# A graph-attention layer on one core: 16 rows a group by the sync engine in place of 8, and another order of the steps of a group

## The chip, the cores and the metric

The kernel runs on one core of a Trainium2 chip. The metric is device time in microseconds (us) of one execution. Three runs of the kernel before gave 2603.59, 2608.92 and 2620.65 us; the median, 2608.92 us, is the number that a change is measured against. One more execution was taken by the hardware profiler. It took 2620.06 us, and all rows, views and stage times below come from it.

The core has five instruction streams that wait for each other through semaphores: TensorE (PE; its weight loads are shown as PEld), VectorE (DVE), ScalarE (ACT), GpSimd (POOL), which issues indirect gathers, and SyncE (SP), which issues plain loads and stores.

## What is computed

The reference is one attention layer over a graph of 12500 nodes with 128 features and 212500 edges that are sorted by their destination, with two normalizations behind it:

```python
Q = (x @ WQ).reshape(N, H, dh)            # N = 12500, H = 8, dh = 16
K = (x @ WK).reshape(N, H, dh)
V = (x @ WV).reshape(N, H, dh)
Eh = (edge_attr @ WE).reshape(-1, H, dh)  # 212500 edges
score = K[src] * Q[dst] / jnp.sqrt(jnp.float32(dh)) * Eh
score = jnp.exp(jnp.clip(score.sum(-1, keepdims=True), -5.0, 5.0))
msg = V[src] * score
wV = jax.ops.segment_sum(msg, dst, num_segments=N)
Z = jax.ops.segment_sum(score, dst, num_segments=N)
h = x + (wV / (Z + ATTN_EPS)).reshape(N, D)
# batch norm of h over the nodes, then layer norm of x + that over the features
```

## The kernel before

**Tiles and stages.** Edges are cut into 1661 tiles of 128, and these into 208 groups of 8 tiles (the last has 5). A group is two half-groups of four tiles, and the destinations of a half lie in a window of 64 nodes, since edges are sorted. The kernel first projects all nodes to a table of K and V in DRAM (`kvd`, one row of 1 KB a node). Then one loop runs over the groups (lines 815 to 865), and a short stage normalizes and stores.

**What a group needs.** K and V rows of its 1024 sources come by indirect gathers on POOL, one per tile of 128 edges (`gather`, line 223), into one of nine slots of SBUF, some eight groups ahead. `load` (line 505) brings the 512 KB of edge features by SP, four groups ahead, into one of three buffers `ea`. Q of the destinations is made by PE from two windows of node columns: `q_window` (ACT copies, line 532), `q_mm` (PE, 563), then `q_hi`, `q_mid`, `q_lo` (ACT, DVE and ACT, DVE), which split the result into three bf16 parts.

**The steps of a group**, with the line of the instruction in the profile:
- `ehqe` (before) projects the edge features, PE line 582 into the PSUM tile `ps_e`, copies them to `wt` by ACT (584), and spreads Q over the edges by six bf16 matmuls, PE 590 into `ps_q`, with the turned one-hot `ot` (DVE 553) as the other operand.
- `both` (DVE 595) multiplies the two; `turn_back` (PE 603, eight transposes into `ps_t`) puts edges on partitions.
- `products` (DVE 616) multiplies with K, `scores` (DVE 623) sums each head, `clip_exp` clips (DVE 631) and makes the exponentials twice on ACT (632 into PSUM, 633 into `msg`).
- `message` (DVE 641) multiplies V with the exponentials; `onehot` (DVE 543, 545, 546) compares destinations with a ramp `iota_ps`; `gather_sum` (PE 656, 657) sums messages by destination; `sums_out` (ACT 662) takes the sums out of PSUM.
- `denom`, `recip`, `attn` (DVE 666, 669, 673) divide; `add_x` (PE 682, 683) adds x; `x_out` (ACT 687) writes the result to the node columns `hx`.

**One PSUM tile is shared.** `small_ps` (`ps_m` in the profile, one bank) holds Q's product, the result of `add_x`, the ramp `iota_ps` and the two sets of exponentials, a quarter each.

**Order.** The schedule is written out by hand: each engine runs its instructions in the order in which the loop calls the steps, for groups from g-3 to g+4 in one pass. Nothing is reordered. A call that must wait holds up all that stands behind it on its engine.

**What paces the gathers.** When `message` has read a slot, `load_kv` queues the gathers of a later group into it. In the next pass `pace` (line 234) lets the first queued gather wait for `q_mm` of that pass, and `issue` gives POOL the rest at once.

**Rows by SP.** The last tile of some groups is not gathered by POOL. SP fetches its 128 rows one at a time: `fetch_rows` (line 271) loads the byte offsets of `SP_ROWS` rows into registers (line 276) and issues as many DMAs of 1 KB (line 283) into a tile `byrow`. It is called in each pass from group 3 on, between the loads and the steps. `row_plan` (line 61) finds which groups get a tile in this way: with 8 rows a group a tile takes 16 groups, and the groups are 20, 36, ..., 196, 12 in all; they gather 7 tiles by POOL. Their last tile has products and messages of its own (`parts`, line 263), behind a wait for the rows (`rows_there`).

Of the kernel before, what the change touches and what calls it, by code (L numbers as in the profile page):

```python
# [8 lines left out]
F32 = mybir.dt.float32  # L9
# [3 lines left out]
AF = mybir.ActivationFunctionType  # L13
# [4 lines left out]
P = 128  # L18
# [4 lines left out]
U = 4  # L23
# [7 lines left out]
FIRST_ROW = 3  # L31
LATE = 8
ROW_LAG = 2
SP_ROWS = 8
WORDS = 4
RQ = 4
NSEM = 6
# [23 lines left out]
def row_plan(sizes):  # L61


    full, n = sizes.count(U) // 2, SP_ROWS
    groups, end = [], P
    while FIRST_ROW + -(-end // n) - 1 + ROW_LAG < full:
        groups.append(max(NX, FIRST_ROW + -(-end // n) - 1 + ROW_LAG))
        end += P
    assert sorted(set(groups)) == groups
    return groups  # L70
# [7 lines left out]
def gnn_kernel(  # L78
# [19 lines left out]
    nc = tc.nc  # L98
# [4 lines left out]
    NG = NW // 2  # L103
# [11 lines left out]
    psp = pps.enter_context(tc.tile_pool(name="psum", bufs=1, space=bass.MemoryType.PSUM))  # L115
# [53 lines left out]
    def load_last():  # L169
        nc.scalar.dma_start(rel_i[:, cut:], dst[:, cut:])  # L170
        nc.scalar.dma_start(srcs[:, cut:], src[:, cut:])
        nc.scalar.dma_start(gb[:, 0:1], gamma)
        nc.scalar.dma_start(gb[:, 1:2], beta)
# [34 lines left out]
    def slot(i):  # L208
        return rows.tile([P, 2 * G * P], F32, name=f"slot{i}")
# [19 lines left out]
    def issue(n=0):  # L229
        while len(queued) > n:  # L230
            f, *a = queued.pop(0)
            f(*a)

    def pace(step):
        if queued:
            f, *a = queued.pop(0)
            tc.add_manual_dep(f(*a).ins, step.ins.name,
                              mybir.DependencyInfo(mybir.DependencyClass.Sync, mybir.DependencyReason.DATA),
                              reason="pace")
# [4 lines left out]
    row_loads = []  # L244
    n = SP_ROWS
    row_tiles = row_plan(usizes)
# [24 lines left out]
    def fetch_rows(g):  # L271
        if g not in fill:
            return
        q = fill[g]
        c = q // P * cols
        _, offs = nc.values_load_multi_w_load_instructions(
            row_ids[q % P:q % P + 1, c:c + cols], engines=(ET.SP,), min_val=0, max_val=(N - 1) * 8 * P,
            skip_runtime_bounds_check_because="node ids")
        for r, off in zip(range(q * n, min(q * n + n, tot)), offs):
            k = row_tiles[r // P]  # L280
            if r % P == 0:
                by_row[k] = rows.tile([P, 1, 2 * P], F32, name="byrow", bufs=2)
            d = nc.sync.dma_start(by_row[k][r % P:r % P + 1, 0, :].bitcast(U8), kvb[ds(off, 8 * P)].unsqueeze(0))
            d.then_inc(rows_in[r // P % NSEM], 16)
            tc.no_tile_sem_insts.add(d.ins.name)
            tc.add_to_no_dep_group(f"rows{k}", d.ins)
# [21 lines left out]
    for g in range(nxg):  # L308
        if g % 2 == 0:
            PAIR[g // 2] = free.pop(0)  # L310
            t = slot(PAIR[g // 2])
# [41 lines left out]
    def within(f, g):  # L353
        return f(g) if 0 <= g < NG else None
# [47 lines left out]
    def load_quad(q):  # L402
        t = late[0].tile([P, RQ, U * P], BF16, name="rbq", bufs=2)
        for h in (0, 1):
            at = ustarts[2 * RQ * q + h] * P
            nc.sync.dma_start(t[h * WN:(h + 1) * WN], bass.AP(
                tensor=relT.tensor, offset=relT.offset + at, ap=[[0, WN], [G * P, RQ], [1, U * P]]))
        for k in range(RQ):
            RB[RQ * q + k] = t[:, k, :]
# [87 lines left out]
    EA, OH, OT, Q3, XW, BASE, MSG, QE, OS, AT, AGG, WT, PW = ({} for _ in range(13))  # L497

    def nt(g):
        return sizes[g]  # L500

    def halves(g):
        return [(0, usizes[2 * g]), (usizes[2 * g], nt(g))]
# [7 lines left out]
    def project_main(g):  # L511

        half = [table_tile(2 * (g % 2) + a) for a in (0, 1)]
        KV[g] = lambda a, b, c, n=P: half[a // 4][:, a % 4:a % 4 + b - a, c:c + n]
        turn_x(g, 0, True)
        turn_x(g, 4, True)
        yield
        for a in (0, 4):
            project(g, a, lambda: turned().rearrange("p (a b) d -> p a (b d)", b=2), True)
            yield  # L520
# [13 lines left out]
    def onehot(g):  # L534


        n, m = usizes[2 * g], usizes[2 * g + 1]
        t = wp.tile([P, U * P + U * WN], F32, name="oh", bufs=2)
        one = t[:, :n * P].rearrange("p (a b) -> p a b", b=P)
        two = t[:, U * P:U * P + m * WN].rearrange("p (a b) -> p a b", b=WN)  # L540
        OH[g] = [one[:, j, :] for j in range(n)] + [two[:, j, :] for j in range(m)]
        r = rel[:, starts[g]:starts[g] + nt(g)]
        nc.vector.tensor_tensor(one, iota_ps[:, None, :].to_broadcast([P, n, P]),  # L543
                                r[:, :n, None].to_broadcast([P, n, P]), op=OP.is_equal)
        nc.vector.tensor_scalar(one[:, :, WN], r[:, :n], lim[:, 2 * g:2 * g + 1], None, op0=OP.is_equal)
        nc.vector.tensor_tensor(two, iota_ps[:, None, :WN].to_broadcast([P, m, WN]),  # L546
                                r[:, n:, None].to_broadcast([P, m, WN]), op=OP.is_equal)
# [26 lines left out]
    def q_lo(g):  # L574
        nc.vector.tensor_sub(Q3[g][:, 2, :], QR[g], Q3[g][:, 1, :])

    def ehqe(g):

        QE[g], WT[g] = [], []
        for a, b in halves(g):  # L580
            eh = psp.tile([P, U * P], F32, name="ps_e", bufs=2)[:, :(b - a) * P]
            nc.tensor.matmul(eh, w_e, EA[g][:, a:b, :].rearrange("p a b -> p (a b)"), start=True, stop=True)  # L582
            t = wp.tile([P, U * P], F32, name="wt", bufs=2)
            nc.scalar.activation(t[:, :(b - a) * P], eh, AF.Copy)  # L584
            WT[g].append(t)
            QE[g].append(psp.tile([P, U * P], F32, name="ps_q", bufs=2)[:, :(b - a) * P])
        for k in range(3):
            for h, (a, b) in enumerate(halves(g)):
                r = slice(h * WN, (h + 1) * WN)
                nc.tensor.matmul(QE[g][h], Q3[g][r, k, :], OT[g][r, :(b - a) * P], start=(k == 0), stop=(k == 2))  # L590

    def both(g, h):
        a, b = halves(g)[h]
        t = WT[g][h][:, :(b - a) * P]
        nc.vector.tensor_tensor(t, t, QE[g][h], op=OP.mult)  # L595
# [165 lines left out]
    q_mid(2)  # L761
    turn_back(0)
    ehqe(1)
    nc.vector.tensor_scalar(row_ids, row_ids, 8 * P, None, op0=OP.mult)
    onehot(0)
    within(load, 2)
    turned_onehot(2)
    load_rel(3)
# [10 lines left out]
    def bn_parts(a, b):  # L779
        for w in range(a, b):  # L780
            for j in due.get(w, []):
                bn_part(j)
                done.add(j)
# [22 lines left out]
    def within_checks(g):  # L806
        if g >= first_check and (g - first_check) % every == 0:
            check((g - first_check) // every)
# [6 lines left out]
    for g in range(NG - 2):  # L815
        within(load, g + 4)
        within(load_rel, g + 5)
        if (g + 6) % RQ == 0 and (g + 6) // RQ in quads:
            load_quad((g + 6) // RQ)
        fetch_rows(g)  # L820
        within(products, g)
        within(both_halves, g + 1)
        step = within(add_x, g - 3)
        step = within(q_mm, g + 3) or step
        if step is not None and queued and g >= LATE + 4:
            pace(step)
        issue()
        within(gather_sum, g - 1)
        if g + 1 < nxg and g + 1 not in SLOT:
            for _ in project_main(g + 1):  # L830
                pass
        within(turn_back, g + 1)
        within(scores, g)
        within(clip_exp, g)
        within(q_hi, g + 3)
        within(x_out, g - 3)
        within(sums_out, g - 1)
        within(q_lo, g + 2)
        within(denom, g - 2)
        within(recip, g - 2)  # L840
        within(attn, g - 2)
        within(q_window, g + 4)
        within(turned_onehot, g + 3)
        within(ehqe, g + 2)
        within(q_mid, g + 3)
        within(message, g)
        within(onehot, g + 1)
        if g == 2:
            load_last()
        for r in runs[1:]:  # L850
            if g == max(4, r[0] // 2 - 12):
                place(r)
        within_checks(g)
        while free and todo and not pending:
            load_x()
        bn_parts(2 * g - 5, 2 * g - 3)
        if g == NG - 5:
            assert done >= set(range(NPRE))
            norm_first()
        if g == LATE - 1:  # L860
            tps.close()
            late.append(tps.enter_context(tc.tile_pool(name="late", bufs=1)))
        if g == LATE - 2:
            free.append(NSLOT)
            load_kv()
    last = NG - 1
    g = last - 1
# [328 lines left out]
```

## Time and profile before

| | |
|---|---|
| median of three runs | 2608.92 us (2603.59 to 2620.65) |
| the profiled execution, own time | 2620.06 us |
| its span, first to last instruction | 2618.3 us |
| mean granted TensorE clock | 0.889 |
| busy: PE, DVE, POOL, ACT | 1833.5, 1659.3, 1589.8, 641.8 us |
| gathers of K and V by POOL | 1585 |
| rows by SP | 1536 |
| first exponential (line 632) to last | 111.8 to 2570.5 us |

A row of the timeline gives the start in us, the time that the instruction or the merged run of instructions took, engine, line, operation, tiles out<-in and a count, and in brackets the idle time of the engine before it with what ended it. A row of the waits gives who waited, for whom, the sum in us, the number of times and the longest. A row of the groups of instructions gives after the count the busy time and the mean ns of one, then the idle time just before them and what ended most of it. A row of the stages gives each engine's busy time in a stretch, the granted clock, the share of the DMA engines' time and GB/s. "remote" and "issue" name waits whose end the profile puts on no engine.

### The profile page before, as it was taken

To read this page: it belongs to the slowest core of one execution; us is meant where nothing else is said; L and a number is where in the kernel's file an instruction comes from. 1 tells how busy PE (TensorE), PEld (TensorE's weight loads), DVE (VectorE), ACT (ScalarE), POOL (GpSimd) and SP (SyncE) were. 2 spreads that over 40 slices of the span, in tenths; PEclk is the share of its full clock that TensorE was granted. 3 is DMA by queue.
4 is the path that set the end of the run, shared out by engine and by line. 5 is a ranking of instruction groups with operands and counts; after the bars stand their busy time and mean duration, and the time that the engine had idled before them with its cause. 6 is when DMAs were issued, how large, how long until landed. Compare 5 with 4: busy or idle time off the path is not lost. (4 is left out here: it accounts for less than half of the span.)

```text
span 2618.3 us, 34368 instructions
## 1 busy us (share of the span) xinstructions
PE 1833.5 (70%) x9414; PEld 1171.7 (45%) x9414; DVE 1659.3 (63%) x3577; ACT 641.8 (25%) x2480; POOL 1589.8 (61%) x1685
## 2 busy tenths in 40 slices
PE   6668676767776676666767677677666776767577
PEld 5445444444444444343444444444434444444346
DVE  2335666666666666666666566666666666666587
ACT  2223222222222222222222222222222222222235
POOL 6644566666666666666666656666666666666524
PEclk8879799888889889999888989988988998799899
DMA  7733444544445444454544544545445454454454
GB/s 229 243 110 110 135 146 147 145 148 145 148 138 154 146 144 148 140 155 137 155 146 138 148 141 144 147 147 145 148 135 155 137 156 137 148 149 140 132 173 118
DMA packets 175392, 386.61 MB, mean 148 GB/s; under 512 B 37518, under 2 KB 91831, under 8 KB 175191
## 3 DMA queue, kind: packets, MB, share of 16 engines
q0 software_dynamic: 78128, 212.05, 27.6%
q1 hardware_dynamic: 92900, 169.50, 21.3%
q10 hardware_dynamic: 4163, 2.78, 0.4%
q8 instruction: 77, 1.26, 0.2%
q14 instruction: 124, 1.02, 0.1%
HBM read 364.57 MB, written 19.63 MB: 147 GB/s over the span
## 5 line engine op out<-in xcount | busy, mean ns | idle before, releaser
L223 POOL DMA_INDIRECT slot<-kvd,srcs x1585 | 1501.3, 947 | 914.6 <-issue 433.2
L657 PE MATMUL ps_a<-msg,oh 128*128 128x136 f32 (+1 forms) x3322 | 609.3, 330 | 5.5 <-issue 4.5
L582 PE MATMUL ps_e<-ea,w_e 128*128 128x512 f32 x832 | 479.6, 648 | 176.5 <-issue 165.5
L657 PEld LDWEIGHTS ps_a<-msg,oh 128*128 128x128 f32 (+1 forms) x3322 | 496.5, 194 | 99.2 <-issue 80.7
L595 DVE TENSOR_TENSOR wt<-wt,ps_q 128x512 f32<-128x512 f32 x416 | 278.2, 685 | 370.7 <-remote 133.8
L632 ACT ACTIVATE ps_m<-s 128x64 f32<-128x64 f32 (+1 forms) x209 | 47.5, 227 | 1497.7 <-PE ps_e L582 541.5
L682 PE MATMUL ps_m<-ident,at 128*128 128x128 f32 x412 | 107.3, 347 | 382.1 <-DVE oh L546 137.6
L603 PE MATMUL ps_t<-ident,wt 128*128 128x128 f32 x1661 | 249.7, 288 | 121.4 <-issue 64.9
L582 PEld LDWEIGHTS ps_e<-ea,w_e 128*128 128x128 f32 x832 | 157.5, 203 | 351.1 <-issue 340.8
L584 ACT ACTIVATE wt<-ps_e 128x512 f32<-128x512 f32 x416 | 236.5, 595 | 249.9 <-PE ps_q L590 130.1
L682 PEld LDWEIGHTS ps_m<-ident,at 128*128 128x128 f32 x412 | 70.1, 213 | 475.6 <-issue 239.3
L571 DVE SCALAR_TENSOR_TENSOR qr<-ps_m,q 128x128 f32<-128x128 f32 x208 | 60.2, 289 | 345.3 <-ACT hx L687 318.6
L616 DVE TENSOR_TENSOR p<-slot,ps_t 128x512 f32<-128x512 f32 (+1 forms) x410 | 259.9, 675 | 19.6 <-remote 13.1
L603 PEld LDWEIGHTS ps_t<-ident,wt 128*128 128x128 f32 x1661 | 194.4, 147 | 152.4 <-issue 77.9
L623 DVE TENSOR_REDUCE s<-p 128x64 f32<-128x1024 f32 (+1 forms) x209 | 252.0, 1206 | 0.1
L641 DVE TENSOR_TENSOR msg<-slot,ps_m 128x1024 f32<-128x1024 f32 (+2 forms) x209 | 246.4, 1181 | 0.4 <-ACT ps_m L632 0.3
L590 PE MATMUL ps_q<-ot,q 64*128 64x512 bf16 x1248 | 177.5, 390 | 5.3 <-issue 5.0
L543 DVE TENSOR_TENSOR oh<-ps_m,rel_i 128x512 f32<-128x512 f32 x208 | 142.2, 684 | 46.7 <-remote 39.8
L590 PEld LDWEIGHTS <-q 64*128 64x128 bf16 x1248 | 46.5, 95 | 199.4 <-issue 175.5
L673 DVE SCALAR_TENSOR_TENSOR at<-os,keep,rz 128x128 f32<-128x128 f32 x208 | 73.3, 352 | 37.2 <-PE ps_t L603 12.0
L563 PE MATMUL ps_m<-w_q,xw 128*128 128x128 f32 x416 | 94.6, 315 | 1.8 <-DVE oh L543 1.6
L687 ACT ACTIVATE hx<-ps_m 128x64 f32 x412 | 90.3, 219 | 8.0 <-PE ps_m L683 1.2
(173 smaller groups left out, 1601.7 us busy)
## 6 DMA issues: line engine op xcount, KB each, us to landing
ea<-eaT SPq DMA_DIRECT2D x207, 512.0 KB
slot<-kvd,srcs POOLq DMA_INDIRECT x1585
byrow<-kvd SPq DMA_DIRECT2D x1536, 1.0 KB
rbq<-relT SPq DMA_DIRECT2D x94, 256.0 KB
kvd<-slot SPq DMA_DIRECT2D x12, 512.0 KB
kvd<-t SPq DMA_DIRECT2D x12, 512.0 KB
slot<-xT SPq DMA_DIRECT2D x24, 256.0 KB
out<-o SPq DMA_DIRECT2D x23, 256.0 KB
```

What stands on the lines that cost most here:

```text
L223: return nc.gpsimd.indirect_dma_start(out=out, out_offset=None, in_=table, in_offset=bass.IndirectOffsetOnAxis(ap=srcs[:, e:e + 1], axis=0))
L543: nc.vector.tensor_tensor(one, iota_ps[:, None, :].to_broadcast([P, n, P]), r[:, :n, None].to_broadcast([P, n, P]), op=OP.is_equal)
L582: nc.tensor.matmul(eh, w_e, EA[g][:, a:b, :].rearrange("p a b -> p (a b)"), start=True, stop=True)
L584: nc.scalar.activation(t[:, :(b - a) * P], eh, AF.Copy)
L590: nc.tensor.matmul(QE[g][h], Q3[g][r, k, :], OT[g][r, :(b - a) * P], start=(k == 0), stop=(k == 2))
L595: nc.vector.tensor_tensor(t, t, QE[g][h], op=OP.mult)
L603: nc.tensor.transpose(ps[:, j, :], WT[g][h][:, j * P:(j + 1) * P], ident)
L616: step = nc.vector.tensor_tensor(PR[g][:, c:d, :], KV[g](c, d, 0), PW[g][i][:, c - a:d - a, :], op=OP.mult)
L623: nc.vector.tensor_reduce(SS[g][:, a:b, :], PR[g][:, a:b, :].rearrange("p t (h d) -> p t h d", d=DH), axis=AX.X, op=OP.add)
L641: step = nc.vector.tensor_tensor(MSG[g][:, a:b, :P].rearrange("p t (h d) -> p t h d", d=DH), KV[g](a, b, P).rearrange("p t (h d) -> p t h ...
L657: nc.tensor.matmul(AGG[g][WN if j >= n else 0:], OH[g][j], MSG[g][:, j, :], start=(j == 0), stop=(j == n - 1))
L682: nc.tensor.matmul(ps, AT[g], ident, start=True, stop=False)
```

## The change

`SP_ROWS` is 16 in place of 8. By `row_plan` a tile is then complete in 8 groups; the groups that have one are 12, 20, ..., 204, 25 in all, and rows are fetched in groups 3 to 202. `ehqe` is cut in three (`eh_mm` on PE, `eh_out` on ACT, `qe_mm` on PE), and the pass calls its steps in another order.

```diff
-SP_ROWS = 8
+SP_ROWS = 16
...
-    def ehqe(g):
-
-        QE[g], WT[g] = [], []
+    EH = {}
+
+    def eh_mm(g):
+
+        EH[g] = []
         for a, b in halves(g):
             eh = psp.tile([P, U * P], F32, name="ps_e", bufs=2)[:, :(b - a) * P]
             nc.tensor.matmul(eh, w_e, EA[g][:, a:b, :].rearrange("p a b -> p (a b)"), start=True, stop=True)
+            EH[g].append(eh)
+
+    def eh_out(g):
+        WT[g] = []
+        for h, (a, b) in enumerate(halves(g)):
             t = wp.tile([P, U * P], F32, name="wt", bufs=2)
-            nc.scalar.activation(t[:, :(b - a) * P], eh, AF.Copy)
+            nc.scalar.activation(t[:, :(b - a) * P], EH[g][h], AF.Copy)
             WT[g].append(t)
-            QE[g].append(psp.tile([P, U * P], F32, name="ps_q", bufs=2)[:, :(b - a) * P])
+
+    def qe_mm(g):
+        QE[g] = [psp.tile([P, U * P], F32, name="ps_q", bufs=2)[:, :(b - a) * P] for a, b in halves(g)]
         for k in range(3):
             for h, (a, b) in enumerate(halves(g)):
                 r = slice(h * WN, (h + 1) * WN)
                 nc.tensor.matmul(QE[g][h], Q3[g][r, k, :], OT[g][r, :(b - a) * P], start=(k == 0), stop=(k == 2))
+
+    def ehqe(g):
+        eh_mm(g)
+        eh_out(g)
+        qe_mm(g)
...
     nc.vector.tensor_scalar(row_ids, row_ids, 8 * P, None, op0=OP.mult)
-    onehot(0)
     within(load, 2)
...
         fetch_rows(g)
         within(products, g)
+        within(q_lo, g + 2)
         within(both_halves, g + 1)
         step = within(add_x, g - 3)
         step = within(q_mm, g + 3) or step
         if step is not None and queued and g >= LATE + 4:
             pace(step)
         issue()
+        within(x_out, g - 3)
+        within(q_window, g + 4)
+        within(q_hi, g + 3)
         within(gather_sum, g - 1)
+        within(eh_mm, g + 2)
         if g + 1 < nxg and g + 1 not in SLOT:
             for _ in project_main(g + 1):
                 pass
         within(turn_back, g + 1)
         within(scores, g)
         within(clip_exp, g)
-        within(q_hi, g + 3)
-        within(x_out, g - 3)
         within(sums_out, g - 1)
-        within(q_lo, g + 2)
         within(denom, g - 2)
         within(recip, g - 2)
         within(attn, g - 2)
-        within(q_window, g + 4)
         within(turned_onehot, g + 3)
-        within(ehqe, g + 2)
+        within(onehot, g)
         within(q_mid, g + 3)
+        within(eh_out, g + 2)
+        within(qe_mm, g + 2)
         within(message, g)
-        within(onehot, g + 1)
+        if g == NG - 3:
+            onehot(g + 1)
```

So on PE the edges' projection stands between `gather_sum` and `turn_back`; on ACT the copies of `x_out`, `q_window` and `q_hi` stand ahead of the exponentials; on DVE the one-hot of a group is made in that group's own pass, ahead of `q_mid` and `message`, and no longer in the pass before, behind `message`; and `q_lo` stands ahead of `both`.

## The prediction

> **What bounds the kernel now.** I read the page's busy times and groups first, then the timelines of POOL, ACT and SP around one pass, then the waits, and last the stages with and without gathers.
>
> ```profile
> PE 1833.5 (70%) x9414; PEld 1171.7 (45%) x9414; DVE 1659.3 (63%) x3577; ACT 641.8 (25%) x2480; POOL 1589.8 (61%) x1685
> ...
> L223 POOL DMA_INDIRECT slot<-kvd,srcs x1585 | 1501.3, 947 | 914.6 <-issue 433.2
> ...
> L595 DVE TENSOR_TENSOR wt<-wt,ps_q 128x512 f32<-128x512 f32 x416 | 278.2, 685 | 370.7 <-remote 133.8
> ```
>
> No engine is full. So the bound is a chain, and the timeline of POOL shows which: eight gathers 1.25 us apart, then a pause; the group with a `byrow` tile has seven.
>
> ```profile
> 1424.02 0.94 POOL L223 DMA_INDIRECT slot<-kvd,srcs  x1 [0.30 <-issue]
> 1427.13 1.00 POOL L223 DMA_INDIRECT slot<-kvd,srcs  x1 [2.17 <-remote]
> 1428.44 0.94 POOL L223 DMA_INDIRECT slot<-kvd,srcs  x1 [0.30 <-issue]
> ...
> 1434.70 0.95 POOL L223 DMA_INDIRECT slot<-kvd,srcs  x1 [0.30 <-issue]
> 1437.52 0.94 POOL L223 DMA_INDIRECT slot<-kvd,srcs  x1 [1.88 <-PE ps_e L582]
> ```
>
> The same three passes on ACT, by the start of the exponential:
>
> ```profile
> 1415.04 0.23 ACT L632 ACTIVATE ps_m<-s 128x64 f32<-128x64 f32 x1 [7.87 <-PE ps_e L582]
> 1426.90 0.23 ACT L632 ACTIVATE ps_m<-s 128x64 f32<-128x64 f32 x1 [7.87 <-PE ps_t L603]
> 1437.28 0.23 ACT L632 ACTIVATE ps_m<-s 128x64 f32<-128x64 f32 x1 [6.47 <-PE ps_e L582]
> 1449.10 0.23 ACT L632 ACTIVATE ps_m<-s 128x64 f32<-128x64 f32 x1 [7.40 <-remote]
> ```
>
> A pass with eight gathers takes 11.86 and 11.82 us, the one with seven 10.38. Over the loop (300.5 to 2507.8 us, 188 passes, by the starts of line 632) the 149 passes with eight gathers have a median of 11.83 us, and 1494 gathers take 2207.3 us, 1.48 us each. POOL and the exponential start 0.23 us apart because both wait for `q_mm`: POOL by `pace`, the exponential because it writes to the same PSUM tile. The record of `q_mm` itself stands 7.6 us earlier (line 563 at 1301.00, exponential at 1308.62). So its completion is seen late, about when the last gather of the burst is through, 2.6 to 2.9 us after that gather's start. The cycle is: `q_mm` seen, burst of gathers, burst through, next `q_mm` seen. Where no gather runs, a pass takes 7.52 us and DVE is full:
>
> ```profile
> 2518.20:2540.70 22.50, 18.91 (x121) 12.27 (x120) 21.84 (x49) 8.17 (x33) 0.00 (x0) 1.00 0.65 207
> 1320.40:1344.10 23.70, 16.40 (x86) 10.53 (x86) 15.35 (x34) 5.41 (x22) 15.13 (x16) 0.93 0.43 134
> ```
>
> The columns after the length are PE, PEld, DVE, ACT and POOL busy, clock, DMA share and GB/s. Compute has over 4 us of air in a pass beside gathers. SP, which is to do twice the rows, shows two speeds:
>
> ```profile
> 1322.91 0.36 SPq L508 DMA_DIRECT2D ea<-eaT  x1
> 1324.15 8.01 SPq L283 DMA_DIRECT2D byrow<-kvd  x8
> 1334.73 0.36 SPq L508 DMA_DIRECT2D ea<-eaT  x1
> ...
> 1485.55 0.36 SPq L508 DMA_DIRECT2D ea<-eaT  x1
> 1485.96 1.25 SPq L406 DMA_DIRECT2D rbq<-relT  x2
> 1488.35 3.68 SPq L283 DMA_DIRECT2D byrow<-kvd  x8
> 1509.24 0.36 SPq L508 DMA_DIRECT2D ea<-eaT  x1
> 1510.49 1.55 SPq L283 DMA_DIRECT2D byrow<-kvd  x5
> ```
>
> In the middle of a burst eight rows take 8.0 us (6.5 and 7.6 in the two passes before), 0.8 to 1.0 each; at the start of one five take 1.55, 0.31 each.
>
> **The change part by part.** The sum is made on the profiled execution's 2620.06 us (span 2618.3), which lies 0.43% over the median of 2608.92; I apply the difference to the median.
>
> *Gathers.* 25 groups in place of 12 have a tile by rows: 13 gathers fewer. One is worth the 1.25 us of POOL's own spacing at least, and at most the 1.48 us of the mean; the difference of the two kinds of pass, 11.83 - 10.38 to 10.51, is 1.32 to 1.45. I take 1.40: 13 x 1.40 = -18.2 us (ends -16.3 and -19.2).
>
> The Trainium skill (DMA: Bandwidth & Descriptors, "Issuing engines are not separate DMA queues") says that DMAs from any engine end on the same 16 DMA engines, and that spreading them saves only issue time. By that the 13 x 128 rows cost as much from SP, and the sum would be 0 in place of -18.2. The seven-gather pass disagrees: its 128 rows are moved too, and it is 1.4 us shorter.
>
> *Rows on SP.* 1664 more row issues, 8 more in each of 192 passes and 16 in 8 more. SP's pass then is one load (0.36), a register load (0.73, perhaps twice that for 16 values), a quarter of 1.25 for `rbq`, and 16 rows. At 0.31 a row that is 6.4 us, at 1.0 a row 17.4. The slow stretch is some 7.1 us of a pass and takes 7 to 9 rows; the other 7 to 9 take 2.2 to 2.8 us. Sum 7.1 + 2.5 + 1.4 = 11.0 us, 11.7 with two register loads. That is under 11.83, so I take nothing, but barely. Behind SP's rows stand the next `ea` load and `rbq`; `ea` is used two passes (23 us) after its issue, and a tile of rows two passes after its last row, so some us of lateness are hidden. If SP needs more than a pass, that cover is used up, and the excess is paid in every pass. The rows' 1 KB transfers I take at nothing, since the pass of 21.3 us at 1492.0 and the others keep the same 1.4 us a gather.
>
> *Edges ahead.* The four records of line 582 move ahead of eight transposes; PE's work is the same. `load` waits for the end of line 582 to free an `ea` buffer (1322.91, 2.5 us after the exponential). Now the transposes no longer stand ahead: 0.8 to 1.6 us earlier. That is the start that SP's sum above needs, and itself worth nothing while SP isn't the bound. The transposes are late by 4 x 0.43 us of PE, where PE waits for DVE 595 in any case.
>
> *ACT.* Two copies of `x_out` (0.47), two of `q_window` (0.40) and `q_hi` (0.26) now run between `q_mm` and the exponential, which so starts 0.9 to 1.3 us after `q_mm` is seen. This is on the way to `message`.
>
> *One-hots and DVE.* `message` starts 1.2 us after the exponential now, and products 3.5. The one-hot (0.68 + 0.23 + 0.42, 1.33 us) leaves the place behind `message`. It reads the ramp in `ps_m`, and waits on that tile go by the whole tile:
>
> ```profile
> PE ps_m L682 <- DVE oh L546: 137.6, 73, 3.4
> ```
>
> PE waits there for a one-hot that reads another quarter. So I take it that the one-hot waits for the exponential. Then exponential until 1.3, one-hot 2.65, `q_mid` 2.95, `message` 4.15: products start 0.65 us later than now. If it needn't wait, 0.6 us earlier. `q_lo` adds 0.28 ahead of `both`. Behind these stands DVE 595, which waits 0.89 us a time now (370.7 / 416), at some 6 us into the pass; the lateness goes there. `q_mm` is issued at about 4.9 us in place of 4.2, and is seen at 11.8 either way: 0. Without that cover it would be +0.65 us a pass, 120 us. The split tiles of 13 more groups add some 0.3 us each on DVE, 4 us, in the same air.
>
> Sum: -18.2 us. 2620.06 becomes 2602 in a profiled execution, and the median 2590.7.
>
> **The rivals.**
>
> *The pause shrinks.* A pass is about 1.41 us a gather and 0.54 us besides (11.83 = 8 x 1.41 + 0.54). In the burst four completions of PE are seen ahead of `q_mm`'s: two of line 590, those of 682 and 683. Edges first and SP at work from early on could let them through sooner, and POOL would not stop. Against it: where POOL ran through, two passes took 7.42 and 21.26 us (exponentials at 1484.6, 1492.0 and 1513.3), 28.7 us for 19 gathers, and the formula gives 27.9. All of it gone: 0.54 x 187 = 101 us, 2490; half, 2540.
>
> *SP becomes the bound.* This one ends slower. If the register load is double and a row in the slow stretch costs 1.0 us, 7 rows fit there, 7.1 + 9 x 0.31 + 2.13 = 12.0, and with waits for line 582 perhaps 12.25: +0.42 us in 175 passes, 73 us, less 18: 2664. It decides from 11.83 us of SP work a pass on. For it: the spread of 6.5 to 8.0 us for 8 rows; against it: SP waits some 2 us a pass for line 582 now.
>
> *The gathers' transfers bound, not their issue.* Then nothing is won: 2609. The seven-gather passes speak against it.
>
> **How the numbers follow.** The forecast (gathers gone, pass unchanged) has 0.43, with a range of its own of 2576 to 2604; the shrinking pause 0.31; SP as the bound 0.18; no effect 0.08. A measurement of this kernel can tell about 1% from no change: 2583 to 2635. Faster by over 1% takes the shrinking pause and 0.05 of the forecast's own range, 0.36; slower takes SP's case and 0.02 of the forecast, for the 0.65 us on DVE where its cover fails, 0.20; within 1% the rest, 0.44. The range leaves out a tenth on each side: from 2525, beyond half the pause, to 2665, SP's price.
>
> **What would show it.** Right: exponentials 11.8 us apart in passes of eight gathers, 25 passes of some 10.4 us, 1572 gathers, products about 4 us after `q_mm` is seen, `ea` loads some 1 us earlier. Wrong: passes of eight gathers under 11.6 us (the pause), or over 12 us with SP issuing rows without a break and `ea` or `byrow` waited for on PE or DVE. A first gather that starts well before the burst ahead of it is through would make my cycle wrong as such.

## The result, and the profile after

The changed kernel took 2738.52 us (median of four executions, 2729.05 to 2744.09) against 2607.14 us for the kernel before (four executions): 1.0489 times, with a 95% interval of 1.0457 to 1.0521. It is slower by 131 us, and outside the range of the prediction. The profiled execution took 2729.05 us (span 2727.3), 109.0 us more span than the profiled execution before.

The page's groups first. Lines are now those of the changed kernel: the exponential is 646, `products` 630, `both` 609, `eh_mm` 584.

```profile
PE 1906.1 (70%) x9414; PEld 1285.0 (47%) x9414; DVE 1659.0 (61%) x3603; ACT 680.0 (25%) x2480; POOL 1575.0 (58%) x1672
...
L223 POOL DMA_INDIRECT slot<-kvd,srcs x1572 | 1486.5, 946 | 1020.5 <-issue 392.9
...
L609 DVE TENSOR_TENSOR wt<-wt,ps_q 128x512 f32<-128x512 f32 x416 | 268.5, 683 | 397.7 <-remote 179.8
...
L630 DVE TENSOR_TENSOR p<-byrow,ps_t 128x128 f32<-128x128 f32 x25 | 7.2, 287 | 222.3 <-DVEq L290 148.2
```

13 gathers are gone (1585 to 1572), yet POOL is idle ahead of them for 1020.5 us in place of 914.6. The last line is new among the costly groups: ahead of the 25 products that read a tile of rows, DVE is idle for 222.3 us, 8.9 us each. Line 290 is the wait for the rows. Before, the 12 such products waited for nothing:

```profile
L616 DVE TENSOR_TENSOR p<-byrow,ps_t 128x128 f32<-128x128 f32 x12 | 3.4, 280 | 0.0
```

One such pass after the change on ACT, by the start of the exponential:

```profile
1357.13 0.23 ACT L646 ACTIVATE ps_m<-s 128x64 f32<-128x64 f32 x1 [1.31 <-DVE rz L680]
...
1369.04 0.23 ACT L646 ACTIVATE ps_m<-s 128x64 f32<-128x64 f32 x1 [1.52 <-DVE s L645]
...
1388.98 0.23 ACT L646 ACTIVATE ps_m<-s 128x64 f32<-128x64 f32 x1 [9.26 <-DVE rz L680]
...
1396.56 0.23 ACT L646 ACTIVATE ps_m<-s 128x64 f32<-128x64 f32 x1 [1.12 <-DVE s L637]
```

11.91 us, then 19.94, then 7.58. DVE in the middle of the long pass:

```profile
1373.76 0.55 DVE L630 TENSOR_TENSOR p<-slot,ps_t 128x384 f32<-128x384 f32 x1 [0.47 <-PE ps_m L696]
1385.84 0.29 DVE L630 TENSOR_TENSOR p<-byrow,ps_t 128x128 f32<-128x128 f32 x1 [11.53 <-DVEq L290]
```

And SP in the same stretch:

```profile
1348.56 11.19 SPq L283 DMA_DIRECT2D byrow<-kvd  x16
1360.47 0.70 SPq L508 DMA_DIRECT2D ea<-eaT  x1
1364.01 11.12 SPq L283 DMA_DIRECT2D byrow<-kvd  x16
1375.16 0.70 SPq L508 DMA_DIRECT2D ea<-eaT  x1
1375.87 1.59 SPq L406 DMA_DIRECT2D rbq<-relT  x2
1378.17 6.31 SPq L283 DMA_DIRECT2D byrow<-kvd  x16
1384.60 0.36 SPq L508 DMA_DIRECT2D ea<-eaT  x1
```

SP works almost without a break (the register loads of line 276, which stand ahead of each 16 rows, are not shown): the row loads end at 1360, 1375 and 1384.5, and 1.4 us after the end of the last of them DVE goes on. SP's own waits say the same. Before, it waited ahead of most `ea` loads (the sum in us, the number of times, the longest):

```profile
SPq L508 <- PE ps_q L590: 266.4, 98, 6.8
SPq L508 <- remote: 224.3, 55, 17.4
SPq L508 <- PE ps_e L582: 110.1, 21, 25.7
```

After, little of that is left:

```profile
SPq L508 <- PE ps_t L340: 34.5, 5, 16.2
SPq L508 <- remote: 26.8, 3, 26.2
...
SPq L508 <- PE ps_e L584: 7.5, 6, 3.6
```

**Where the time went.** I count a long pass and the one behind it together, since the second gives back what gathers the first had time for. The 25 pairs take 684.7 us and hold 372 gathers. By the prediction's formula (1.41 us a gather and 0.54 a pass) they would take 552 us: 133 us too much. Less the 18 us of the gathers saved that is +115; from the first exponential to the last it is +108.8 (2567.5 against 2458.7). The other passes, without the first twelve of the loop and the last five, have hardly changed: a median of 11.83 us as before, a mean of 11.75 in place of 11.65. So nearly all of the loss lies in the passes that use rows.

SP's pass is counted from one register load (line 276) to the next, as a mean without the first twelve and the last three, and its rows from the end of the register load to the end of the last row. Before it is 11.78 us, of which the rows take 6.97 and SP is idle ahead of the `ea` load for 3.14. After it is 12.31 us, rows 10.09, idle 0.19. So SP's work a pass went from 8.64 to 12.12 us, which is more than the pass that the gathers need. 200 passes of 0.53 us more are 106 us: the same loss, counted at SP.

### The profile page after: what moved, and what is told of

Its sections match the earlier page's. It is cut to its first block, busy times and chain, and to the rows that moved or that the text cites. A ratio compares the mean times of both kernels' runs of the same rounds, so it can differ in the third digit from the quotient of the medians.

```text
span 2727.3 us, 37937 instructions
## 1 busy us (share of the span) xinstructions
PE 1906.1 (70%) x9414; PEld 1285.0 (47%) x9414; DVE 1659.0 (61%) x3603; ACT 680.0 (25%) x2480; POOL 1575.0 (58%) x1672
## 4 chain that ended last, share of the span: by engine, by line
DVE 25%; PE 24%; issue 22%; SPq 13%; another core or an unknown queue 10%; ACT 3%; DMA 2%; POOL 1%; DVEq 1%; ACTq 0%; POOLq 0%
SPq L283 10%; PE ps_a L671 10%; DVE s L637 5%; DVE wt L609 4%; PE ps_e L584 3%; DVE msg L655 3%; DVE oh L543 3%; PE ps_m L696 2%; DVE ot L553 2%; DVE p L630 2%; ACT wt L591 2%; PE ps_m L563 1%; SPq L276 1%; PE ps_a L670 1%
## 5 line engine op out<-in xcount | busy, mean ns | idle before, releaser
L223 POOL DMA_INDIRECT slot<-kvd,srcs x1572 | 1486.5, 946 | 1020.5 <-issue 392.9
L671 PE MATMUL ps_a<-msg,oh 128*128 128x136 f32 (+1 forms) x3322 | 706.4, 367 | 27.3 <-issue 20.6
L671 PEld LDWEIGHTS ps_a<-msg,oh 128*128 128x128 f32 (+1 forms) x3322 | 580.3, 221 | 140.0 <-issue 120.4
L696 PE MATMUL ps_m<-ident,at 128*128 128x128 f32 x412 | 119.0, 378 | 464.0 <-ACT wt L591 159.3
L584 PE MATMUL ps_e<-ea,w_e 128*128 128x512 f32 x832 | 411.4, 613 | 44.2 <-DMA ea<-eaT 24.7
L617 PEld LDWEIGHTS ps_t<-ident,wt 128*128 128x128 f32 x1661 | 209.1, 152 | 309.7 <-issue 143.6
L599 PE MATMUL ps_q<-ot,q 64*128 64x512 bf16 x1248 | 190.0, 411 | 5.5 <-issue 5.4
L572 ACT ACTIVATE q<-qr 128x128 bf16<-128x128 f32 x208 | 64.3, 309 | 349.7 <-DVE qr L571 182.9
L630 DVE TENSOR_TENSOR p<-byrow,ps_t 128x128 f32<-128x128 f32 x25 | 7.2, 287 | 222.3 <-DVEq L290 148.2
L563 PE MATMUL ps_m<-w_q,xw 128*128 128x128 f32 x416 | 105.6, 345 | 9.8 <-issue 7.9
L697 PE MATMUL ps_m<-xw,ident 128*128 128x128 f32 x412 | 101.8, 337 | 5.0 <-issue 5.0
```

The lines of the kernel that those rows point to most:

```text
L223: return nc.gpsimd.indirect_dma_start(out=out, out_offset=None, in_=table, in_offset=bass.IndirectOffsetOnAxis(ap=srcs[:, e:e + 1], axis=0))
L617: nc.tensor.transpose(ps[:, j, :], WT[g][h][:, j * P:(j + 1) * P], ident)
L630: step = nc.vector.tensor_tensor(PR[g][:, c:d, :], KV[g](c, d, 0), PW[g][i][:, c - a:d - a, :], op=OP.mult)
L671: nc.tensor.matmul(AGG[g][WN if j >= n else 0:], OH[g][j], MSG[g][:, j, :], start=(j == 0), stop=(j == n - 1))
L696: nc.tensor.matmul(ps, AT[g], ident, start=True, stop=False)
```

## The experiments

The theory is **SP's sum of a pass**. 16 row loads make SP's pass longer than the pass of eight gathers (11.84 us), the lateness adds up over the eight groups that fill a tile, and DVE pays it at the tile's product. The rivals are: the rows come a fixed time late (they lack a lead); a row tile costs by itself (its bytes, its parts on DVE); the new order costs.

Each ratio compares with the kernel before on the same chip. The chips turned out to be of two kinds. On the first kind, that of the two profiles above too, the kernel before takes 2607 to 2621 us; on the second it takes 2123. The runs e5 to e8 and g1 to g3 were on the second kind, all others on the first.

**The order alone, and the rows alone.** The change with `SP_ROWS = 8` (e1), and the kernel before with 16 (e2):

```diff
-SP_ROWS = 16
+SP_ROWS = 8
```

> The changed kernel with SP_ROWS back at 8, so the new order alone. Theory (SP has more work than a pass lasts, and vector work waits for rows that come late): with 8 rows SP needs 8.6 us of an 11.8 us pass, as before, so nothing waits for rows, and the time is that of before, 2607 us, within 15. Rival (the order delays the exponential and the products, and that is the loss): 2607 + 65 to 130, so 2670 to 2738 us.

> The kernel before with SP_ROWS 16, so the rows alone in the old order. Theory: SP is overloaded as in the changed kernel, 2720 to 2760 us, with VectorE waiting about 200 us for rows in 25 groups. Rival (the order is the loss): 13 gathers fewer at 1.4 us, 2590 us.

Measured: e1 2632.99 us, 1.0045 (1.0028 to 1.0062); e2 2796.52 us, 1.0677 (1.0655 to 1.0700). The loss comes with the rows, and in the old order it is larger than the 2720 to 2760 us that I expected. The new order takes part of it back, to 1.0489, and costs 0.45% without them. The granted TensorE clock explains little of it: it is 0.859 to 0.889 in the runs of the kernel before on this kind of chip and 0.811 to 0.829 in those of the change, but e1, which loses 0.45%, has 0.831 to 0.838, and f2 below, which loses nothing, 0.837 to 0.851.

**12 rows** (the change with `SP_ROWS = 12`).

> The changed kernel with 12 rows a pass: 18 groups with a tile by rows, 6 gathers fewer than before. Theory: SP needs 8.6 us plus four rows at 0.5 to 0.9, so 10.6 to 12.2 us of an 11.8 us pass; it just fits, nothing or little waits for rows, 2595 to 2615 us. Rival (order): 2665 to 2735 us. If the loss grew evenly with the rows, half of it would show: 2670 us.

Measured: 2646.03 us, 1.0101 (1.0083 to 1.0119). 18 tiles of rows are used and DVE waits for none of them:

```profile
L630 DVE TENSOR_TENSOR p<-byrow,ps_t 128x128 f32<-128x128 f32 x18 | 5.1, 281 | 0.0
```

SP's pass is 11.92 us with 0.59 idle. So the loss does not grow evenly with the rows; it sets in between 12 and 16, where SP's idle time ends. The gain I expected isn't there either: this kernel is 0.56% behind the order alone, though it has 6 gathers fewer. Its exponentials start 2.41 us after the burst's first gather, in place of 1.15, and its passes of eight gathers, from burst to burst, take 12.06 us in the mean in place of 11.95. This second lateness goes with the number of row loads in a pass: with 8 on SP alone (e1, f2) the median is 1.15 and 1.13 us, and with 12 or 16 it is 2.39 to 2.41, in the old order too (e2; with 8 rows the old order's exponential starts 0.23 us ahead of the gather) and where ScalarE issues part of them (h1, h2). In these runs `both` starts 0.33 us ahead of a burst, thus only when the burst ahead is through, and in e1 2.4 us ahead of it; why, no run isolates.

**More lead** (the change with a tile used six groups after its last row, not two).

```diff
-ROW_LAG = 2
+ROW_LAG = 6
```

> The changed kernel with ROW_LAG 6 in place of 2, so a tile of rows is used four passes later. Theory (SP's work is more than a pass, so it falls behind by 1 to 2 us in every pass): four passes, 47 us, of slack are used up once and the loss goes on after that, partly as waits for the load of edge features; 2685 to 2730 us. Rival (each tile's last rows are only some 10 us late in landing, a fixed lateness): all of the loss is gone, 2590 us.

Measured: 2752.88 us, 1.0515 (1.0490 to 1.0539). No wait for rows is left among DVE's, and nothing is won, not even what I expected from the longer slack (2685 to 2730 us), because the lateness turns up at the load that stands behind the rows:

```profile
L584 PE MATMUL ps_e<-ea,w_e 128*128 128x512 f32 x832 | 634.0, 904 | 547.2 <-DMA ea<-eaT 447.5 <-issue 78.1 <-ACT q L572 14.5
```

PE now waits 447.5 us for the edge features (24.7 in the change), and the passes without row products take 12.50 us in the mean in place of 11.65. A missing lead is ruled out: SP can't do the work in the time of a pass, and the order of its queue only chooses who pays.

**Half the issues, the edge load on another queue, the edges' place, and 4 rows: on the second kind of chip.** e5 fills 16 rows by 8 loads, each of which writes one source row into two partitions, and leaves out the row that belongs in the second (the wait for the rows counts half as many loads):

```diff
-        for r, off in zip(range(q * n, min(q * n + n, tot)), offs):
+        for r, off in list(zip(range(q * n, min(q * n + n, tot)), offs))[::2]:
...
-            d = nc.sync.dma_start(by_row[k][r % P:r % P + 1, 0, :].bitcast(U8), kvb[ds(off, 8 * P)].unsqueeze(0))
+            d = nc.sync.dma_start(by_row[k][r % P:r % P + 2, 0, :].bitcast(U8),
+                                  kvb[ds(off, 8 * P)].unsqueeze(0).to_broadcast([2, 8 * P]))
...
```

e6 issues the edge loads by ScalarE's queue, e7 puts the edge projection back behind the turning back, e8 is the kernel before with `SP_ROWS = 4`:

```diff
-        nc.sync.dma_start(EA[g][:, :n, :].rearrange("p a b -> p (a b)"),
+        (nc.scalar if g >= 5 else nc.sync).dma_start(EA[g][:, :n, :].rearrange("p a b -> p (a b)"),
```

```diff
-        within(eh_mm, g + 2)
         if g + 1 < nxg and g + 1 not in SLOT:
...
+        within(eh_mm, g + 2)
         within(eh_out, g + 2)
```

> The changed kernel with 16 rows a group filled by 8 row loads: each load writes one source row into two partitions (half of the row tile's contents are wrong, so the output is not the reference's). The row tiles, the gathers (13 fewer than before), the parts on VectorE and the semaphore waits stay those of the change; SP's row issues are halved, to 8 a pass. Theory 'SP's sum of a pass is over the gathers' 11.84 us': SP is idle again in each pass, VectorE's waits for rows are gone, and the time is that of the order alone less the gathers saved, 2633 - 13 x 1.41 = 2615 us, between 2600 and 2635. Rival 'a row tile costs by itself' (its bytes, its parts on VectorE, its wait): 2700 to 2740 us as with 16 loads.

> The changed kernel with the edge load of each group from group 5 on issued by ScalarE's queue instead of SP's; the 16 row loads stay on SP. Theory 'SP's sum': SP's pass goes from 12.55 us (mean) to about 12.55 - 0.70 - 0.4 = 11.4 us, under the gathers' 11.84, so the lateness no longer collects: the waits for rows on VectorE shrink from 209 us to under 60 us and the time is 2620 to 2670 us. Rival 'SP's pace beside the gathers is not a sum but stretches to fill the pass': no gain, 2720 to 2745 us.

> The changed kernel with the edge projection put back behind the next group's turning back (all else of the change stays: 16 rows, one-hots later, the add of x and the q window moved). If the edges ahead are what made the change (ratio 1.049) better than 16 rows in the old order (1.068), the time is near 2790 us; if the one-hots or the other moves did it, it stays at 2735 to 2750 us.

> The kernel before with 4 rows a group in place of 8: 6 row tiles fewer, so 6 gathers more. If row loads on SP cost nothing beside gathers as long as SP keeps up, the gathers cost 6 x 1.41 = 8.5 us: 2629 us, ratio 1.003. If each row load already slows the pass that it lies in, this kernel is as fast as before or faster (2600 to 2620 us).

Measured: 2117.18 us, 0.9975 (0.9965 to 0.9984); 2119.74, 0.9982 (0.9973 to 0.9992); 2108.76, 0.9935 (0.9920 to 0.9950); 2129.93, 1.0032 (1.0020 to 1.0045). The expected times don't fit, because the chip is another, and none of the theories for 16 rows can be told apart here, since nothing is lost. e8's ratio is as expected (1.003). SP in e7, which has the full 16 row loads:

```profile
1349.92 5.09 SPq L283 DMA_DIRECT2D byrow<-kvd  x16
1355.69 0.36 SPq L508 DMA_DIRECT2D ea<-eaT  x1
1357.38 5.09 SPq L283 DMA_DIRECT2D byrow<-kvd  x16
```

and POOL in the same microseconds:

```profile
1350.08 0.95 POOL L223 DMA_INDIRECT slot<-kvd,srcs  x1 [0.30 <-issue]
1351.33 0.94 POOL L223 DMA_INDIRECT slot<-kvd,srcs  x1 [0.30 <-DMA slot<-kvd,srcs]
1352.58 0.95 POOL L223 DMA_INDIRECT slot<-kvd,srcs  x1 [0.30 <-issue]
```

Gathers are issued all the while, and 16 rows take 5.09 us, 0.32 each. SP has room (it waits 430.6 us for line 584), no row is late, and 16 rows are worth what the gathers saved are: 13 x 1.25 = 16 us are 0.77% of 2123, e7 gained 0.65%. So in these runs 16 rows lose only on the kind of chip on which SP's steps are slow beside gathers. The order's cost seems to lie in the edges' place here: e7, with the edges put back, gains 0.65%, and the variants with 16 rows and the edges ahead (e5, e6 and below g1, g2) gain 0.18 to 0.33%; the change itself wasn't run on this chip.

**The change and the first three of these again, on the first kind of chip.**

> The change itself, as the mark for the runs beside it. On the chip of the first four runs a row load took SP 0.70 us or more while gathers were issued and the kernel before took 2621 us; on the chip of the last four it took 0.32 us beside the gathers too, and the kernel before took 2123 us. Theory 'SP's sum, stretched beside the gathers': on a chip of the first kind 1.045 to 1.055 times before; on one of the second kind SP's pass is about 8 us, under any pass of 8 gathers, and the change is 0.990 to 0.998 times before (13 gathers of 1.25 us saved is 16 us of 2123). Rival 'the rows or the order cost by themselves': slower by 4 to 5% on both.

> The changed kernel with 16 rows a group filled by 8 row loads, each of which writes one source row into two partitions (half of the row tile's contents are wrong). On a chip of the first kind (a row load 0.70 us beside gathers), theory 'SP's sum': SP is idle again, 0.99 to 1.005 times before, so some 120 us under the change beside it; rival 'a row tile costs by itself': as slow as the change. On a chip of the second kind it is within 0.5% of the change, since SP has room with 16 loads too.

> The changed kernel with the edge load of each group from group 5 on issued by ScalarE's queue. On a chip of the first kind, theory 'SP's sum': SP's pass goes from 12.55 us to about 11.4 us, under the gathers' 11.84; 1.000 to 1.020 times before, the waits for rows on VectorE under 60 us. Rival 'SP stretches to fill the pass': as slow as the change, 1.045 to 1.055. On a chip of the second kind: within 0.5% of the change.

> The changed kernel with the edge projection put back behind the next group's turning back. On a chip of the first kind: if the edges ahead are what made the change better (1.049) than 16 rows in the old order (1.068), 1.06 to 1.07 times before; if the one-hots or the other moves did it, 1.045 to 1.055. On a chip of the second kind the same kernel took 0.9935 times before: if the edges ahead cost something there, the change beside it is slower than that by about 0.5%.

Measured:

| kernel | us | ratio (95%) | SP's pass, rows, idle before `ea` (us, means) | DVE idle before row products (us) |
|---|---|---|---|---|
| f1, the change | 2743.43 | 1.0522 (1.0487 to 1.0557) | 12.38, 10.17, 0.20 | 225.9 |
| f2, half the issues | 2579.93 | 0.9890 (0.9859 to 0.9922) | 11.59, 6.55, 2.75 | 0.0 |
| f3, edge load by ScalarE | 2700.01 | 1.0348 (1.0315 to 1.0381) | 12.24, 10.62, none | 160.9 |
| f4, edges not ahead | 2738.70 | 1.0498 (1.0462 to 1.0534) | 12.39, 10.17, 0.21 | 262.4 |

f2 has the same 25 row tiles, the same number of bytes in them, the same parts on DVE, and half of SP's loads: the whole loss is gone, 163 us. "A row tile costs by itself" falls.

f3 came out between the two theories. One load and its wait were taken from SP and the rows took longer in return (10.62 for 10.17), so that its pass shrank by 0.14 us and not by 1.1. Without the `ea` load SP runs through:

```profile
1350.31 11.10 SPq L283 DMA_DIRECT2D byrow<-kvd  x16
1363.05 1.53 SPq L406 DMA_DIRECT2D rbq<-relT  x2
1367.38 34.41 SPq L283 DMA_DIRECT2D byrow<-kvd  x57
```

57 loads in 34.41 us, 0.60 each. The row loads and the register loads alone (10.62 and 0.89 us in the mean) are about a pass. f3 doesn't settle how far a row load stretches to fill the pass. f4 is as fast as the change: the edges' place neither costs nor wins anything that shows here, so what took e2's 1.068 back to 1.049 is among the other moves, not isolated.

**The rows on two queues.** Is it the queue, or the number of row transfers? 16 rows a group, of which ScalarE issues 4 (g1, h1) or 8 (g2, h2); and the old order with half the issues (g3, h3).

```diff
-            row_ids[q % P:q % P + 1, c:c + cols], engines=(ET.SP,), min_val=0, max_val=(N - 1) * 8 * P,
+            row_ids[q % P:q % P + 1, c:c + cols], engines=(ET.SP, ET.Activation), min_val=0, max_val=(N - 1) * 8 * P,
...
-            d = nc.sync.dma_start(by_row[k][r % P:r % P + 1, 0, :].bitcast(U8), kvb[ds(off, 8 * P)].unsqueeze(0))
+            d = (nc.scalar if r % 4 == 3 else nc.sync).dma_start(by_row[k][r % P:r % P + 1, 0, :].bitcast(U8), kvb[ds(off, 8 * P)].unsqueeze(0))
```

> The changed kernel, 16 row loads a group, of which SP issues 12 and ScalarE 4 (ahead of the copies of x, where ScalarE waits 3.9 to 4.6 us a pass now; 4 loads of 0.70 us and the register load of 0.9 us are 3.7 us). On a chip where a row load takes SP 0.70 us beside gathers: theory 'SP's queue is full': SP's pass has room again as with 12 rows (11.92 us), the waits for rows are mostly gone, and with 13 gathers fewer the time is 0.990 to 1.010 times before. Rival 'the number of row transfers': 1.04 to 1.055 as the change. On a chip where it takes 0.32 us: 0.990 to 1.000.

> The changed kernel, 16 row loads a group, 8 by SP and 8 by ScalarE. On a chip where a row load takes 0.70 us beside gathers, SP is idle some 3 us a pass as before and no row is late for SP's sake; ScalarE spends 8 x 0.70 + 0.9 = 6.5 us ahead of its copies of x where it waited 3.9 to 4.6, so its exponentials come some 2 us later: 1.00 to 1.15 times before, by how far that is on the path; the waits for rows on VectorE are gone under the theory 'SP's queue is full', and stay near 200 us under the rival 'the number of row transfers'. On a chip where it takes 0.32 us: 0.990 to 1.000.

> The kernel before, in its own order, with 16 rows a group filled by 8 row loads, each of which writes one source row into two partitions (half of the row tile's contents are wrong): 13 gathers fewer for the same number of SP issues. By the formula of a pass, 13 x 1.40 = 18 us less: 0.993 times before on a chip with the pause between bursts. If the new order costs what the order alone showed (0.45%), it is some 12 us under the changed kernel with halved loads (0.989), so near 0.985; if the halved loads gained for another reason that lies in the order, 0.993 or more. On a chip without the pause: 13 x 1.25 = 16 us of 2123, 0.992.

These fell on the second kind of chip: 0.9977 (0.9966 to 0.9989), 0.9967 (0.9955 to 0.9979) and 0.9929 (0.9911 to 0.9947), as expected there, and they separate nothing but the order: 0.9975 (e5) against 0.9929 (g3), both with half the issues, says that it costs 0.46% there. On the first kind:

> The changed kernel, 16 row loads a group, 12 issued by SP and 4 by ScalarE. On a chip where a row load takes SP 0.70 us beside gathers: theory 'SP's queue is full': SP has room again as with 12 rows (11.92 us a pass), VectorE's waits for rows fall from 226 us to under 60, 0.990 to 1.010 times before. Rival 'the number of row transfers': 1.04 to 1.055 as the change.

> The changed kernel, 16 row loads a group, 8 by SP and 8 by ScalarE. On a chip where a row load takes 0.70 us beside gathers: VectorE's waits for rows are gone under 'SP's queue is full' and stay near 200 us under 'the number of row transfers'; ScalarE spends 6.5 us ahead of its copies of x where it waited 3.9 to 4.6, so 1.00 to 1.15 times before, by how far that is on the path.

> The kernel before in its own order, 16 rows a group filled by 8 row loads (each writes one source row into two partitions; half of the row tile's contents are wrong). On a chip with the pause between bursts: 13 x 1.40 = 18 us less than before, 0.993; 0.985 if the new order's 0.45% comes off the 0.989 of the changed order with halved loads; 0.993 or more if that 0.989 is partly the new order's gain.

Measured: h1 2626.13 us, 1.0054 (1.0036 to 1.0071); h2 2616.96 us, 1.0003 (0.9983 to 1.0023); h3 2592.07 us, 0.9929 (0.9898 to 0.9960). With the same 3200 row transfers DVE waits for no row any more, in h1 as in h2; the line of h1:

```profile
L630 DVE TENSOR_TENSOR p<-byrow,ps_t 128x128 f32<-128x128 f32 x25 | 7.0, 279 | 0.0
```

So the full queue of SP is the cause, not the transfers. Neither split beats the kernel before. What the 13 gathers save (0.7%) is lost again; ScalarE's queue and the later exponentials (2.41 us after the burst's first gather in h1, as in e3) are where it may go, but no run separates them. ScalarE in h1 between two groups' copies:

```profile
1362.09 0.60 ACT L591 ACTIVATE wt<-ps_e 128x512 f32<-128x512 f32 x1 [2.88 <-remote]
1363.42 1.44 ACTq L283 DMA_DIRECT2D byrow<-kvd  x4
1365.21 0.48 ACT L701 ACTIVATE hx<-ps_m 128x64 f32 x2 [2.52 <-PE ps_e L584]
```

h3 is the term of the gathers by itself, with what a row tile costs on DVE: 0.9929 of 2613.14 us is 18.6 us less (10 to 27 by the interval), and the prediction had 18.2.

## Why the prediction was wrong

- **Gathers: right.** 1572 gathers, and with SP's issues kept at 8 the 13 gathers are worth 0.71% on the first kind of chip (h3). The Trainium skill's rule that I weighed there (DMA: Bandwidth & Descriptors, "Issuing engines are not separate DMA queues") would have given 0; the rows' transfers cost nothing that shows. But the same section calls the time saved on the issuing sequencer "usually small relative to the DMA itself", and here that time is the whole case: h1 and f1 differ in the queue of a quarter of the row issues only (with a register load for them on ScalarE), and their ratios, on two chips of the first kind, by 4.7 points.
- **Rows on SP: the step that failed.** It said "7.1 + 2.5 + 1.4 = 11.0 us, 11.7 with two register loads. That is under 11.83, so I take nothing, but barely." Measured: 12.31, of which SP was idle for 0.19. The sum was made the right way, and two of its terms were too small. The 16 rows took 10.09 us and not 9.6: from 3 to 10.5 us after a burst's first gather a row load took 1.04 us in the mean, near the 0.8 to 1.0 of the sum, but all others took 0.40 and not 0.31. What is left took 2.22 us and not 1.4. The three steps that were priced came to 1.36 us as forecast (register load 0.86, `ea` 0.31, `rbq` 0.19); the time between them and in the semaphore instructions, 0.67 us (0.23 before), and the 0.19 idle were put at nothing. The register load did not double in the mean (0.79 before, 0.86 after). In the changed kernel 605 of the 3000 spacings between the row loads of a pass are over 1.2 us, and 1621 under 0.5. The same in one subtraction: the 8 added rows cost SP 12.12 - 8.64 = 3.5 us a pass, and the sum gave them 2.5.
- **The cover: right in kind.** "If SP needs more than a pass, that cover is used up, and the excess is paid in every pass" is what happens, but it is paid at the row tile, once in eight passes, and the sum is about 0.53 us x 200.
- **The rival "SP becomes the bound": right in kind, too cheap.** It had 12.25 us a pass, measured 12.31, and 175 passes; it came to 2664. All 200 passes with rows pay, and against the mean pass of 11.78, not against 11.83 with the seven-gather passes as slack. The margin that the forecast rested on was 0.1 to 0.8 us of a sum whose ends, at 0.31 and 1.0 us a row, lay 11 us apart: 0.18 was too little for it.
- **Edges ahead: 0, right** (f4 against f1, on the first kind of chip), but not for the reason given: the `ea` loads could not come earlier, since SP was hardly ever free.
- **ACT order and one-hots: right in size for the order, and nearly in effect.** With the order alone (e1) the exponential starts 1.15 us after the burst's first gather (0.9 to 1.3 expected) and products 4.73 (about 4). In the change itself they start at 2.41 and 5.98 us, and `q_mm` is issued at 7.2 (4.9 expected); that second part comes with the row loads, as said at e3. The one-hot does wait for the exponential, though ten times only:

```profile
DVE oh L543 <- ACT ps_m L646: 31.7, 10, 9.5
```

  Nearly all of this lateness lay under the burst, as the prediction had it: the passes of eight gathers have a median of 11.84 us. The order alone cost 0.45% (e1), which the forecast had at 0; from burst to burst its passes of eight gathers take 11.95 us in the mean against 11.90 before, some 9 of the 12 us. With half the issues the new order was no worse than the old on the first kind of chip (0.9890 against 0.9929, intervals that meet), so its price there is not settled.
- **The pause did not shrink**: 2.14 us without a gather in the median before, 2.17 after. **Transfers bound, not issue**: excluded by h3.
- **Two readings were off, without weight in the sum.** From 300.5 to 2507.8 us the record has 187 passes and 1482 gathers, 1.49 us each (188, 1494 and 1.48 in the prediction). SP waited 3.14 us a pass ahead of the `ea` load and not some 2; line 582 is named for 110 of 666 us in all.

## What to carry to other kernels

Before an idle queue is given more work, sum its whole pass at the prices that its steps have beside the busiest neighbour, every step and not only the added one, and take the margin against the spread of these prices. Where such a queue fills up, more lead only moves the wait to the next load behind it. A small gain that hangs on issue times should be looked at on more than one chip: here the same edit was 5% slower on one kind and no slower in any variant with 16 rows that was run on the other (the change itself wasn't run there).

## What the runs showed of the hardware

- On the first kind of chip SP's steps are slow while POOL issues gathers: 16 row loads take 11.1 us beside them, 5.1 on the second kind. From 1359.04 to 1365.41 us of the changed kernel the steps start 0.70 to 0.73 us apart or twice that, but for some that follow at once, whether they are moves, DMA issues, the `ea` load or the register load. Even a move between SP's registers, 29 ns in the median, takes up to 1.4 us; minimum, median and maximum in ns stand behind the count (tile `byrow` of the changed kernel):

```profile
L283 SPq MOVE byrow<-kvd x3200: 1/29/1402, 150.9 to 2653.0; - x189
L283 SPq DMA_DIRECT2D byrow<-kvd x3200: 1/228/1400, 150.9 to 2653.1; - x189
```

- The end of a matmul is also seen late there. With one and the same kernel the copy of Q's product (line 567) starts 5.38 us after the end of `q_mm` in the median on the first kind (f4), and 1.04 us on the second (e7). With it goes the pause between the bursts: POOL is idle 1032.3 us ahead of its gathers in f4 and 479.2 in e7, and in the old order 914.6 us before against 485.0 in e8 (1591 gathers):

```profile
L223 POOL DMA_INDIRECT slot<-kvd,srcs x1591 | 1508.7, 948 | 485.0 <-issue 421.0
```

- A gather takes POOL the same on both (948 and 947 ns). The second kind runs the kernel before in 2123 us, 19% less. Its granted TensorE clock is higher too (0.90 to 0.93 in these runs against 0.80 to 0.89). What in the chip makes the difference stays open.
